# Two-layer transformer: the attention's division queued beside one set of transposes, the next set moved to every second slot

## The chip, the cores and the metric

The kernel runs on one core of a Trainium2 chip. The metric is the device time of one execution in microseconds (us). The core has a matrix engine (TensorE, PE in the profile; its weight loads are listed apart as PEld), a vector engine (VectorE, DVE), a scalar engine (ScalarE, ACT), a general engine (GpSimd, POOL) and a queue for transfers (SyncE, SP). Each engine runs its own list of instructions, and they wait for one another through semaphores.

## The reference, cut to what matters

Four residual steps, each behind a layer norm, over four sequences of 512 positions and 256 features:

```python
x = x + attention0(layernorm(x))      # causal, 16 heads of 16
x = x + mixture0(layernorm(x))        # 8 experts, the best two of each output feature, weighted
x = x + attention1(layernorm(x))      # 16 heads of 128, 4 key heads
x = x + ffn1(layernorm(x))            # gelu(gate) * up, then down, weights of 4 bits
```

The change concerns the first of them:

```python
qkv = einsum('bsd,od->bso', x, w_project)          # then split into q, k, v by head
att = einsum('bhqd,bhkd->bhqk', q, k) / sqrt(16)
att = where(causal, -1e9, att)                     # no key after the query
att = softmax(att, axis=-1)
out = einsum('bhqk,bhkd->bhqd', att, v)
out = einsum('bsd,od->bso', out (heads joined), w_out)
```

The softmax's sum is not taken before the mixing. The values carry a column of ones, so the mixed values come with their own denominators, and the division is made at the end, once for each head and query.

## The kernel before, in words

**Tiling.** The residual `xres` stays on chip as 16 tiles of 128 rows by 256 features. Attention of layer 0 goes by blocks `j` = 0 to 3; a block holds 128 query positions of each of four sequences `s`, and its queries meet the keys of blocks 0 to `j`. Heads are taken four at a time, in groups `g` = 0 to 3. A *batch* is one `(j, s)` with some of its groups: all four in block 0, two in block 1, one in blocks 2 and 3. That makes 4 + 8 + 16 + 16 = 44 batches, numbered `n`.

**What a batch does.** `greatest` (matmuls L614) makes the scores of one batch, `mask` (L629) adds the causal mask to them by matmul and takes each row's greatest on VectorE (L634). `shift` transposes the maxima on TensorE (L645) and subtracts them from the queries on VectorE (L650). `powers` (L664) makes the scores again, transposed, from the shifted queries; ScalarE takes the exponentials (L673) and GpSimd clears what the mask forbids (L683). `mixed` (L700) multiplies with the values, and ScalarE copies the result into `avs` (L708).

**The order of the main work.** The loop over batches writes, for each `n`: scores of `n + 1`, shift of `n`, mask of `n + 1`; a slot; mix of `n - 1`, powers of `n`; a slot.

**The slots.** Everything else is put into these slots by a small planner, `fill`. Each call adds one to the counter `slot` and gives budgets, in microseconds by the author's reckoning, for TensorE and VectorE: 4.0, 2.0, 1.8 or 1.6 for TensorE in the first slot of a batch by block, 4.0, 2.4, 2.2 or 2.0 in the second, and 2.6 for VectorE in each. A budget that was overdrawn is carried on as a debt; one that was left over is not. The other work is a list of *streams*, Python generators. Each piece begins with `yield need(engine, cost, gap, cond)`: it runs once its engine's budget is above zero, `gap` slots have passed since the stream's last piece, and `cond`, if there is one, holds. The streams are asked in the order of the list, again and again, until none can go. The order in which the pieces are written is the order in which TensorE, VectorE and GpSimd carry them out, for their order is taken from the program. At the last batch of a block, slots are added until the next block's inputs are ready, if they are not; after the last batch, slots with 2.0 and 2.6 follow until the last stream of `divided` is done.

**The streams of layer 0.** `prepare` (norm, transposes, projections and values of the next block; its queries and keys go through `stage` and eight transfers into `qk`), `divided` (below), `fold_pieces` (biases folded into router and expert weights `rw` and `ew`), `hidden_pieces` (the norm and the transposes ahead of the mixture), `logit_pieces` and `result_pieces` (the router's and the experts' matmuls, `lg_ps` and `eo`, L226), `weight_pieces` and `addition_pieces` (the mixture's weights and sums on VectorE). What is left of the mixture when layer 0's attention ends goes into the slots of layer 1.

**`divided(j, s)`** is put at the head of the list after the powers of the batch that follows the last batch of `(j, s)`, and so runs 16 times. Its pieces: four transposes of `avs` on TensorE into the PSUM tile `av_T` (L718), which puts the queries on the partitions; a slot later the reciprocal of the denominators (L724) and the product with them (L725), which give `oq`; a slot later two transposes of `oq` into `oq_T` (L733) and ScalarE's copy into `aT` (L736). After the last sequence of a block come the output's matmuls (L745) and the addition to the residual (L754) for two pairs of tiles, and `hidden_pieces(j)` is added to the list.

**PSUM.** Layer 0's scores take turns in five buffers (`ps_sc`), the maxima and the mixed values in one (`ps_mm`). All that the streams make on TensorE takes turns in two buffers, `ps_dn`, with the tag `dn`. A buffer is held until the last reader of its tile is written down in the program, and whoever takes it next waits until that reader is done.

Of the kernel before, what the change touches and what calls it, by code (L numbers as in the profile page):

```python
# [32 lines left out]
def tile_transformer(  # L33
# [75 lines left out]
    slot = 0  # L109

    def need(engine, cost, gap=0, cond=None):
        return engine, cost, gap, cond
# [25 lines left out]
    left = {"PE": 0.0, "DVE": 0.0}  # L138
# [117 lines left out]
    def hidden_pieces(b):  # L256

        out = []
        done = (4 * b - 5, 1)
        last = b == NBLK - 1  # L260
        yield from norm_pieces(b, b1, b2, out, cond=lambda: b < 2 or done in halves)
        xT = b2.tile([P, 2, 512], F32, tag="xT", name=f"xT{b}")
        for hc in range(2):
            yield need("PE", 0.5, 0 if hc else 1 + last)
            ps = transposed(out[0], hc, ps_dn, "dn", f"xT_ps{b}_{hc}")
            ps = ps.rearrange("p t q -> p (t q)")
            if hc:
                nc.scalar.activation(xT[:, hc, :], ps, AF.Identity, bias=last_16)
            else:
                nc.scalar.copy(xT[:, hc, :], ps)  # L270
        normed.clear()
        xTs[b] = xT
# [159 lines left out]
    with ExitStack() as l0:  # L432
# [279 lines left out]
        def divided(j, s):  # L712

            yield need("PE", 0.5, 1)
            avs = avs_of.pop((j, s))
            ps = ps_dn.tile([P, NH0, 32], F32, tag="dn", name=f"av_T{j}_{s}")
            for g in range(4):
                nc.tensor.transpose(  # L718
                    ps[:, 4 * g : 4 * g + 4].rearrange("p h d -> p (h d)"), avs[:, g], ident
                )  # L720
            rden = a2.tile([P, NH0], F32, tag="rden", name=f"rden_{j}_{s}")
            oq = a1.tile([P, NH0, 16], F32, tag="oq", name=f"oq_{j}_{s}")
            yield need("DVE", 0.7, 1)
            nc.vector.reciprocal(rden, ps[:, :, 16])  # L724
            nc.vector.tensor_tensor(  # L725
                oq, ps[:, :, 0:16], rden.unsqueeze(2).to_broadcast([P, NH0, 16]), ALU.mult
            )
            yield need("PE", 0.3, 1)
            if not s:
                aTs[j] = a1.tile([P, 2, 16, NS, 8], F32, tag="aT", name=f"aT{j}")  # L730
            ps = ps_dn.tile([P, 2, P], F32, tag="dn", name=f"oq_T{j}_{s}")
            for k in range(2):
                nc.tensor.transpose(  # L733
                    ps[:, k], oq[:, 8 * k : 8 * k + 8].rearrange("p h d -> p (h d)"), ident
                )
            nc.scalar.copy(aTs[j][:, :, :, s, :], ps.rearrange("p k (g b) -> p k g b", b=8))  # L736
            if s < NS - 1:
                return

            for t in (0, 2):  # L740
                yield need("PE", 1.75, 1)
                ps = ps_dn.tile([P, 2, HID], F32, tag="dn", name=f"o0_{j}_{t}")
                for i in range(2):
                    for k in range(2):
                        nc.tensor.matmul(  # L745
                            ps[:, i],
                            lhsT=aTs[j][:, k, 4 * (t + i) : 4 * (t + i) + 4].rearrange(
                                "p g s b -> p (g s b)"
                            ),
                            rhs=wo[:, k, :], start=k == 0, stop=k == 1,  # L750
                        )
                yield need("DVE", 0.7, 1)
                both = xres[:, 4 * j + t : 4 * j + t + 2, :]
                nc.vector.tensor_tensor(both, both, ps, ALU.add)  # L754
            fold_at = streams.index(fold) if fold in streams else len(streams) - 4
            streams.insert(fold_at, Stream(hidden_pieces(j)))
# [19 lines left out]
        for n in range(NBT):  # L776
# [19 lines left out]
            if n and batches[n - 1][2][-1] == 3:  # L796
                streams.insert(0, Stream(divided(*batches[n - 1][:2])))
# [10 lines left out]
        mixed(NBT - 1)  # L808
        streams.insert(0, Stream(norm_pieces(0, b1, b2, normed_first)))
        last = Stream(divided(*batches[NBT - 1][:2]))  # L810
        streams.insert(0, last)
        while last.next is not None:
# [442 lines left out]
```

## Time and profile before

| | |
|---|---|
| Median of 3 runs | 1215.86 us (1215.13 to 1215.92) |
| The profiled execution's own time | 1213.42 us |
| Its span | 1211.7 us |
| Mean clock granted to TensorE | 0.989 |
| TensorE busy | 1168.9 us, 96% |
| VectorE busy | 802.6 us, 66% |
| ScalarE busy | 485.5 us, 40% |
| GpSimd busy | 121.1 us, 10% |
| L718, transposes of `avs` | 64 matmuls, 10.6 us, 287 ns each |
| L724, reciprocal | 16 times, 4.0 us, 250 ns each |
| L725, product | 16 times, 6.8 us, 424 ns each |
| L733, transposes of `oq` | 32 matmuls, 6.8 us, 293 ns each |
| L736, copy into `aT` | 16 times, 6.4 us, 400 ns each |

The span goes from the first instruction to the last; the profiled execution's own time is a little longer than the span. Layer 0's attention takes the time up to about 420 us. In a row of the timeline, the numbers are the start, the length, then engine, line, operation and the tile written and read, and how many instructions were merged; in brackets stands how long the engine was idle ahead of it, and what ended that. A busy time adds up the recorded lengths. Where TensorE waits in the midst of a group of matmuls, the group's length can grow, and no idle time is shown.

### The profile page before, as it was taken

To read this page: it belongs to the slowest core of one execution; us is meant where nothing else is said; L and a number is where in the kernel's file an instruction comes from. 1 tells how busy PE (TensorE), PEld (TensorE's weight loads), DVE (VectorE), ACT (ScalarE), POOL (GpSimd) and SP (SyncE) were. 2 spreads that over 40 slices of the span, in tenths; PEclk is the share of its full clock that TensorE was granted. 3 is DMA by queue.
4 is the path that set the end of the run, shared out by engine and by line. 5 is a ranking of instruction groups with operands and counts; after the bars stand their busy time and mean duration, and the time that the engine had idled before them with its cause. 6 is when DMAs were issued, how large, how long until landed. Compare 5 with 4: busy or idle time off the path is not lost.

```text
span 1211.7 us, 18780 instructions
## 1 busy us (share of the span) xinstructions
PE 1168.9 (96%) x7278; PEld 679.8 (56%) x7278; DVE 802.6 (66%) x1780; ACT 485.5 (40%) x1101; POOL 121.1 (10%) x155
## 2 busy tenths in 40 slices
PE   6979999999999898999999999999999999999998
PEld 3656555555555543555555555656645456475487
DVE  2555589898887848737886395798499853735710
ACT  1233455664555444434444345355344321312300
POOL 8333321121111000000000000000000000000000
PEclk9899999999999998999999999999999999999999
DMA  7122102000000040000000001021020000000000
GB/s 221 17 56 54 19 4 34 2 1 1 2 1 2 27 147 1 1 1 1 1 1 1 1 1 36 10 55 43 1 62 9 1 1 17 1 1 18 0 1 35
DMA packets 21305, 26.78 MB, mean 22 GB/s; under 512 B 5120, under 2 KB 14592, under 8 KB 21216
## 3 DMA queue, kind: packets, MB, share of 16 engines
q1 hardware_dynamic: 20544, 24.40, 7.6%
q10 hardware_dynamic: 672, 1.18, 0.4%
q8 instruction: 57, 0.93, 0.3%
q14 instruction: 32, 0.26, 0.1%
HBM read 19.27 MB, written 2.10 MB: 18 GB/s over the span
## 4 chain that ended last, share of the span: by engine, by line
PE 81%; DVE 12%; ACT 2%; DMA 2%; issue 1%; SPq 1%; POOL 0%; ACTq 0%; DVEq 0%; POOLq 0%
PE qk_ps L928 10%; PE o L1019 9%; PE y L1175 9%; PE g L856 8%; PE u L856 8%; PE eo L226 8%; PE lg_ps L226 7%; PE s L614 4%; DVE mx L634 3%; PE s L664 3%; PE av L700 2%; PE v_ps L910 2%; PE qk_ps L529 2%; PE s L941 1%; PE a L999 1%
## 5 line engine op out<-in xcount | busy, mean ns | idle before, releaser
L928 PE MATMUL qk_ps<-xT,wqkv 128*128 128x512 f32 x320 | 148.7, 599 | 0.6 <-ACT qT L932 0.6
L226 PE MATMUL lg_ps<-rw,xT 128*128 128x512 f32 x256 | 123.8, 607 | 3.7 <-ACT xT L895 1.7
L226 PE MATMUL eo<-ew,xT 128*128 128x512 f32 x256 | 122.0, 600 | 1.3 <-ACT part L315 1.0
L1019 PE MATMUL o<-wpj,oT 128*128 128x256 f32 x512 | 119.8, 382 | 0.0
L634 DVE TENSOR_REDUCE mx<-s 128x1 f32<-128x384 f32 (+3 forms) x176 | 100.5, 634 | 20.3 <-PE s L629 20.3
L1175 PE MATMUL y<-wd,it 128*128 128x256 f32 x512 | 111.8, 379 | 0.0
L1019 PEld LDWEIGHTS o<-wpj,oT 128*128 128x128 f32 x512 | 95.9, 190 | 28.1 <-issue 15.1
L1175 PEld LDWEIGHTS y<-wd,it 128*128 128x128 f32 x512 | 97.1, 190 | 14.9 <-issue 2.2
L928 PEld LDWEIGHTS qk_ps<-xT,wqkv 128*128 128x128 f32 x320 | 59.3, 190 | 70.0 <-issue 60.2
L673 ACT ACTIVATE pt<-s 128x512 f32<-128x512 f32 (+1 forms) x176 | 83.7, 561 | 34.4 <-PE s L664 34.3
L856 PE MATMUL g<-xT,wgu 128*128 128x512 f32 x192 | 90.4, 593 | 0.0
L856 PE MATMUL u<-xT,wgu 128*128 128x512 f32 x192 | 90.2, 592 | 0.0
L315 ACT ACTIVATE part<-eo,c 128x256 f32<-128x256 f32 x128 | 53.7, 473 | 81.5 <-PE eo L226 76.9
L683 POOL TENSOR_SCALAR_AFFINE_SELECT pt<-pt 128x256 f32<-128x256 f32 (+2 forms) x88 | 55.2, 632 | 268.6 <-ACT pt L673 268.1
L1153 ACT ACTIVATE th<-sq 128x512 f32<-128x512 f32 x64 | 40.3, 629 | 87.6 <-DVE sq L1152 87.6
L177 POOL TENSOR_TENSOR ln_rs<-rs_v,minus_half 128x4 f32<-128x4 f32 x16 | 18.0, 1127 | 563.3 <-DVE rs_v L176 457.9
L226 PEld LDWEIGHTS lg_ps<-rw,xT 128*128 128x128 f32 x256 | 46.5, 192 | 49.0 <-issue 36.9
L226 PEld LDWEIGHTS eo<-ew,xT 128*128 128x128 f32 x256 | 46.4, 190 | 45.8 <-issue 37.0
L614 PE MATMUL s<-qk 32*128 32x128 f32 (+3 forms) x512 | 69.7, 478 | 1.3 <-DMA qk<-stage 0.5
L214 DVE TENSOR_TENSOR xres<-xres,y 128x256 f32<-128x256 f32 x16 | 6.7, 421 | 92.2 <-PE y L1175 92.2
L650 DVE TENSOR_TENSOR qk<-qk,mxT 128x128 f32<-128x128 f32 (+2 forms) x44 | 15.2, 346 | 77.0 <-PE mxT L645 69.3
L289 ACT COPY lg<-lg_ps 128x512 f32<-128x512 f32 x64 | 37.6, 587 | 64.5 <-PE lg_ps L226 64.3
(233 smaller groups left out, 1831.2 us busy)
## 6 DMA issues: line engine op xcount, KB each, us to landing
qk<-stage SPq DMA_DIRECT2D x56, 64.0 KB, 2.4
wqkv<-in_w_qkv SPq DMA_DIRECT2D x8, 320.0 KB, 6.0
rw<-in_router_w SPq DMA_DIRECT2D x8, 256.0 KB, 4.8
ew<-in_expert_w SPq DMA_DIRECT2D x8, 256.0 KB, 5.0
wpj<-in_w_proj SPq DMA_DIRECT2D x1, 2048.0 KB, 11.9
out<-xres SPq DMA_DIRECT2D x4, 512.0 KB, 2.6
xres<-in_x SPq DMA_DIRECT2D x3, 512.0 KB, 8.1
dq_wgu<-in_gate_w SPq DMA_DIRECT2D x8, 128.0 KB, 2.4
```

The lines of the kernel that those rows point to most:

```text
L226: nc.tensor.matmul(ps, lhsT=xT[:, hc, (g % 4) * P : (g % 4 + 1) * P], rhs=w[:, hc, 2 * pair : 2 * pair + 2, :].rearrange("p e o -> p (e o) ...
L289: nc.scalar.copy(lg[:, 2 * pair : 2 * pair + 2, :].rearrange("p e o -> p (e o)"), ps)
L315: nc.scalar.mul(part[:, e % 4], ps[:, i], c[:, e : e + 1])
L614: nc.tensor.matmul(tiles[h][:, b * nk : (b + 1) * nk].rearrange("p (c k) -> p c k", k=P), lhsT=queries(j, g)[r, s], rhs=qk[r, g, : j + 1, ...
L634: nc.vector.tensor_reduce(maxes[n % 2][:, :nb, h, 0], ps[:, : nb * nk].rearrange("p (b k) -> p b k", b=nb), AX.X, ALU.max,)
L673: nc.scalar.activation(pt[:, i, : nb * nk], tiles[2 * pair + i][:, : nb * nk], AF.Exp, scale=0.25)
L683: nc.gpsimd.affine_select(out=last, in_=last, compare_op=ALU.is_ge, fill=0.0, base=0, pattern=pattern, channel_multiplier=-1,)
L856: nc.tensor.matmul(ps, lhsT=wgu[:, w, half, jj, par * P : (par + 1) * P], rhs=xT[:, half, :], start=half == 0, stop=half == 1,)
L928: nc.tensor.matmul(ps, lhsT=wqkv[:, hc, kv, h, :], rhs=xT[:, hc, :], start=hc == 0, stop=hc == 1,)
L1019: nc.tensor.matmul(ys[t // 2][:, t % 2], lhsT=state["o"][:, h, t * P : (t + 1) * P], rhs=wpj[:, HPK * kv + h, :], start=kv == 0 and h == 0 ...
L1153: nc.scalar.activation(th, sq, AF.Tanh, scale=0.7978845608028654)
L1175: nc.tensor.matmul(ps, lhsT=it[:, c // 2, c % 2, t * P : (t + 1) * P], rhs=wd[:, c // 2, c % 2, :], start=c == 0, stop=c == 2 * NJ - 1,)
```

## The change

In `divided`, three lines differ. The piece that made the division no longer yields: reciprocal and product are written down directly behind the transposes of `avs`, in the same slot, and 0.7 is taken off VectorE's budget by hand, so that the budget may go below zero. The piece with the transposes of `oq` keeps its cost of 0.3 and its gap of one slot, counted now from the transposes of `avs`, and gets a condition: the number of the slot has to be odd. Since the counter begins at 0, the first slot of the first batch, behind a mask, has the number 1.

```diff
                 nc.tensor.transpose(
                     ps[:, 4 * g : 4 * g + 4].rearrange("p h d -> p (h d)"), avs[:, g], ident
                 )
+
             rden = a2.tile([P, NH0], F32, tag="rden", name=f"rden_{j}_{s}")
             oq = a1.tile([P, NH0, 16], F32, tag="oq", name=f"oq_{j}_{s}")
-            yield need("DVE", 0.7, 1)
+            left["DVE"] -= 0.7
             nc.vector.reciprocal(rden, ps[:, :, 16])
             nc.vector.tensor_tensor(
                 oq, ps[:, :, 0:16], rden.unsqueeze(2).to_broadcast([P, NH0, 16]), ALU.mult
             )
-            yield need("PE", 0.3, 1)
+
+            yield need("PE", 0.3, 1, cond=lambda: slot % 2)
             if not s:
                 aTs[j] = a1.tile([P, 2, 16, NS, 8], F32, tag="aT", name=f"aT{j}")
```

## The prediction

> **What bounds the kernel now.** I read the page's totals first, then the busy time by stretch of layer 0, then TensorE's timeline with the idle time ahead of each row, last VectorE's rows around the same moments.
>
> ```profile
> PE 1168.9 (96%) x7278; PEld 679.8 (56%) x7278; DVE 802.6 (66%) x1780; ACT 485.5 (40%) x1101; POOL 121.1 (10%) x155
> ...
> PE 81%; DVE 12%; ACT 2%; DMA 2%; issue 1%; SPq 1%; POOL 0%; ACTq 0%; DVEq 0%; POOLq 0%
> ```
>
> TensorE sets the end: 1168.9 of 1211.7 us busy and 81% of the chain. No matmul is removed, so what can shrink or grow is its idle 42.8 us, and waits that hide inside stretched rows. Where that idle time lies (columns: stretch, length, busy time of PE, PEld, DVE, ACT, POOL, granted clock, DMA share, GB/s):
>
> ```profile
> 42.00:92.00 50.00, 40.54 (x481) 27.71 (x480) 28.75 (x55) 16.58 (x32) 18.00 (x16) 0.94 0.20 43
> 92.00:162.00 70.00, 66.03 (x784) 41.27 (x786) 40.26 (x86) 29.22 (x60) 24.67 (x26) 0.97 0.15 32
> 162.00:290.00 128.00, 123.89 (x1252) 68.03 (x1245) 112.68 (x287) 72.19 (x205) 21.65 (x35) 1.00 0.06 10
> 290.00:427.00 137.00, 132.29 (x1285) 72.93 (x1282) 115.30 (x273) 70.34 (x184) 17.11 (x32) 0.99 0.05 15
> ```
>
> The four stretches in which the edited helper runs hold 9.5, 4.0, 4.1 and 4.7 us of idle PE. TensorE's timeline, picked rows (start, length, row, idle before it and what ended it):
>
> ```profile
> 64.60 0.66 PE L718 MATMUL av_T<-ident,avs 128*128 128x128 f32 x4
> 65.09 0.38 PE L733 MATMUL oq_T<-ident,oq 128*128 128x128 f32 x2
> 67.13 1.99 PE L529 MATMUL qk_ps<-xT,wp 128*128 128x512 f32 x4 [1.65 <-ACT aT L736]
> ...
> 84.03 0.44 PE L733 MATMUL oq_T<-ident,oq 128*128 128x128 f32 x2 [1.81 <-DVE oq L725]
> 84.93 0.38 PE L244 MATMUL fold<-rows 128*128 128x512 bf16 x1 [0.46 <-ACT aT L736]
> ...
> 114.67 0.38 PE L244 MATMUL fold<-rows 128*128 128x512 bf16 x1 [1.30 <-DVE oq L725]
> ...
> 199.41 0.66 PE L202 MATMUL xT_ps<-ident,xn 128*128 128x128 f32 x4 [1.23 <-ACT aT L736]
> ```
>
> Two sorts of wait. At 84.03 the divided values' transposes wait for a late division: on VectorE it stands behind four reductions and four batch-norm pairs, and ends at 83.97. At 67.13 and 114.67 a matmul that does not read the division waits for a buffer. The pool `dn` has two. `av_T` keeps one from its transposes until the division, which is emitted a slot later; everything emitted between runs through the other one alone, each product waiting for the evacuation of the last. At 67.13 the projection could take only the buffer of `oq_T`, so it waited for the copy `aT`.
>
> **What the Trainium skill says.** PSUM — Partial Sum Buffer, section Engine vs sequencer instructions: VectorE's queue is strictly first in, first out, and matmuls complete in program order; the trace agrees (the division at 83.27 comes after all eight batch-norm rows, though its data were there at 82.2). The same page, Specifications (TRN2): eight banks per partition; score 5, `mm` 1 and `dn` 2 are all of them, so no third `dn` buffer relieves this. Perfetto Trace Analysis, section Optimization Strategy: a gap that repeats on the engine that should be full can mean no buffer for the next tile; idle times of 0.68, 0.67, 0.68 and 0.67 at 51.60, 58.63, 91.22 and 93.01 fit. TensorE: Matmul & The Clock Gate, section What's actually happening: idling for a window of about 3.4 us halves the array's clock; here the clock is 0.50 from 86 to 94, where one group of 32 `av` matmuls took 1.94 us against 1.08; but the longest single gap before it is 1.81, so the trace agrees in kind only.
>
> **The change, part by part.** Each batch has two slots: the first (odd number) behind the mask, the second (even) behind the powers. The count starts at 0, and the loops at block ends add no slot in the order the trace shows, so parity holds through all 44 batches. Before, a group's av_T goes into even slot k, its division into k+1, its oq_T into k+2. Now the division is queued in k and oq_T goes into k+1. The last group (slots 89, 90, 91) keeps its place, since 90 is even: 15 of 16 move.
>
> *Removed waits, 42 to 100 us.* Buffer: 0.68 (51.60), 0.67 (58.63), 1.65 (67.13) = 3.00. Late: 0.16 + 0.56 (74.67, 75.86), 1.81 + 0.46 (84.03, 84.93), 1.31 (89.46), 0.68 (91.22), 0.67 (93.01), 0.38 (99.40) = 6.03. Not all can be kept. The scores at 76.20 need eight transfers whose queries leave at 69.1 and land near 76; the projection moves by 3.00, so I allow 3.0 there, and the 0.72 at 74.67 and 75.86 is lost to the transfers. Next VectorE limits: from the shift at 78.21 to that at 89.23 it works nearly without a gap. The same work in the new order (reductions 2.4, statistics 2.2, rs_v 0.2, fold 1.3, division 0.7, normalising 3.5) saves only the 0.58 wait for POOL, which fold and division now cover. So 3.0 + 0.6 + 0.68 + 0.38, and half of 0.67: 5.0 kept of 9.0.
>
> *92 to 162 us.* 1.30 at 114.67 goes (VectorE idles 3.71 before the shift at 111.18, so the division can run at once). Of 0.68 + 0.78 + 0.16 at 130 to 132 I take half, since oq_T joins that crowded slot: 2.1.
>
> *162 to 410 us.* At 164.80 powers waited 1.80 for the shift, which stood behind VectorE's filler. The division's 0.7 is now debited one slot earlier, so one 1.22 us subtraction leaves that slot: 1.22 - 0.67 = 0.5. Further 0.25 (167.38), 1.23 (199.41), twice 0.16: 2.3. The wait of 0.73 at 410.86 is the last group's and stays.
>
> *Added.* oq_T (0.44 a pair) lay behind the powers, where scalar exponentials still hold the score buffers that the next scores need; its time there was partly free. Score groups of block 3 take 1.14 us undisturbed, but 3.21, 2.42, 3.16 and 3.35 at 305.34, 315.15, 363.73 and 389.43: the wait is inside the row. Of the seven pairs from 197 to 388, two stand ahead of such stretched groups and others are near: 3 x 0.44 = 1.3. In slot 24 the 0.3 of planner budget set free lets one more product in early, and slot 26 loses one, so its scores meet the exponentials uncovered: 0.7, an estimate from these stretches.
>
> *At nothing.* VectorE does the same work. The division (0.25 + 0.42) now waits at the head of its slot for av_T; behind it stand that slot's filler, the next shift and its reductions. A stall there is covered by VectorE's wait for the next maxima's transpose: in 10 of the 15 cases VectorE sat idle before that shift (7.31, 6.93, 2.50, 3.71, 2.88, 5.05, 2.66, 0.60, 2.17, 2.11 us). In the other five, cover gone, it costs at most 0.67 each = 3.4, less what the earlier debit holds back; I take 0, and keep -3.4 in the range. The copy `aT` (0.41) moves ahead of the exponentials, where ScalarE is mostly idle. No DMA is added; those behind the projections leave earlier by what these move. Output products and hidden(0) may start a slot earlier, but folded weights and first products stay bound to slot 19; layer 1 gets the same work.
>
> Sum: -5.0 - 2.1 - 2.3 + 1.3 + 0.7 = -7.4 us. Against the profiled execution's own 1213.42 (span 1211.7) that is 1206.0. The shown runs' median is 2.4 higher: 1215.86 - 7.4 = 1208.5.
>
> **Rivals.** *More is kept, and the clock stays up.* Idle PE around 84 to 92 costs the half clock for 10.2 us; in it av (+0.86), mask (+0.45), two normed transposes (+0.88), powers (+0.37) and small rows (+0.7) lost 3.3. With 2 of the 4.0 withheld also kept: 1208.5 - 5.3 = 1203. For: two waits of that gap go. Against: the normalised rows themselves stay VectorE's.
>
> *Hidden anyway.* Transfers to 76 and VectorE's run to 89 hold the early start, and the later exposures eat the rest: 1215.
>
> *Slower.* oq_T comes out from under the exponentials in all 15 groups: 15 x 0.44 = 6.6, while the early stretch gives back only about 3.5: 1219. It decides once exposed time passes the kept waits. Against: 10 of the 14 score groups from 161 to 259 take their undisturbed 0.93, so there is no wait there to pay unless they stood within 0.44 of one.
>
> *It doesn't do what it says.* If parity flipped at a block end, oq_T would stay in its old slot and only the buffer part (about 3) would come: 1212.5.
>
> **How the numbers follow.** Likeliest 0.60, with 1205.5 to 1212 as its own range; the larger gain 0.17; parity 0.03; hidden 0.12; slower 0.08. Measurement tells about 0.2% = 2.4 us from nothing. Faster: 0.60 + 0.17 + 0.03 = 0.80; same 0.12; slower 0.08. The range 1202.5 to 1215.0 holds the likeliest, most of the larger gain and a part of hidden.
>
> **What would show it.** Right: division rows next to av_T on VectorE, before the shift; no PE wait on oq at 84 and 114; the projection after av_T at full pace; oq_T after mask rows; idle PE in 42 to 92 near 5 instead of 9.5. Wrong: new PE waits of powers on the shift, score groups stretched behind the groups' powers, or the transfers' wait growing near 73 to 76. Another half-clock stretch elsewhere (3.3 each) would also break the number.

## The result, and the profile after

The median fell from 1215.49 us to 1204.49 us (six runs of each): ratio 0.9924, with a 95% interval of 0.9898 to 0.995. The same kernel, run again beside the experiments, had 1205.89 us against 1212.61: 0.995 (0.9934 to 0.9966). The profiled execution took 1203.68 us with a span of 1202.0 and a mean clock of 0.993, where before had 1213.42, 1211.7 and 0.989. The two profiles differ by 9.7 us.

The page after, its totals and the shares of the chain by engine:

```profile
PE 1161.8 (97%) x7278; PEld 676.9 (56%) x7278; DVE 804.8 (67%) x1780; ACT 488.4 (41%) x1101; POOL 124.2 (10%) x155
...
PE 82%; DVE 11%; DMA 2%; ACT 2%; issue 1%; POOL 0%; SPq 0%; ACTq 0%; DVEq 0%; POOLq 0%
```

TensorE still sets the end. Its idle time went from 42.8 us to 1202.0 - 1161.8 = 40.2, and its 7278 matmuls take 7.1 us less, so that most of the gain lies inside rows, not between them (1.0 of it in the six matmuls ahead of the first batch, which took 5.46 and 4.48 us). A row is also longer where the granted clock is lower, and before ran at half clock for longer; what that makes is estimated below, at the rival on the clock. The busy time by stretch, in the columns used before:

```profile
42.00:92.00 50.00, 46.89 (x561) 32.45 (x558) 28.01 (x56) 20.78 (x40) 18.62 (x17) 0.97 0.20 44
92.00:162.00 70.00, 66.16 (x776) 41.89 (x773) 48.51 (x105) 30.61 (x65) 25.23 (x25) 1.00 0.12 24
162.00:290.00 128.00, 126.70 (x1285) 69.59 (x1288) 113.21 (x280) 72.65 (x203) 21.87 (x35) 1.00 0.06 10
290.00:427.00 137.00, 125.69 (x1193) 67.56 (x1185) 110.99 (x275) 73.57 (x195) 16.45 (x28) 1.00 0.12 40
```

In the first stretch TensorE is idle for 3.1 us instead of 9.5, and 561 matmuls end in it instead of 481; in the third for 1.3 instead of 4.1. The last line can't be set beside before's: by then the kernel is ahead, and the stretch reaches into the start of layer 1 (its share of transfers rose from 15 to 40 GB/s).

The timeline of TensorE after, picked rows (start, length, row, idle time before it and what ended that):

```profile
52.69 3.62 PE L551 MATMUL v_ps<-wp,xT 128*128 128x256 f32 x16
...
60.29 0.66 PE L718 MATMUL av_T<-ident,avs 128*128 128x128 f32 x4
61.84 1.96 PE L529 MATMUL qk_ps<-xT,wp 128*128 128x512 f32 x4 [0.90 <-DVE oq L726]
...
78.87 0.61 PE L629 MATMUL s<-later,ident_h 128*128 128x128 bf16 x8
79.62 0.44 PE L735 MATMUL oq_T<-ident,oq 128*128 128x128 f32 x2
80.40 0.30 PE L202 MATMUL x_ps<-ident,xn 128*128 128x128 f32 x1 [0.34 <-DVE xn L186]
82.20 1.89 PE L202 MATMUL x_ps<-ident,xn 128*128 128x128 f32 x7 [1.50 <-DVE xn L186]
...
388.80 1.08 PE L700 MATMUL av<-pt,va 128*32 128x128 f32 x32 [1.34 <-DVE qk L650]
...
393.93 2.52 PE L700 MATMUL av<-pt,va 128*32 128x128 f32 x32 [1.03 <-ACT pt L673]
...
407.49 1.99 PE L747 MATMUL o<-wo,aT 128*128 128x256 f32 x8 [1.06 <-DVE xres L756]
```

The lines of the edited helper now have other numbers: division L725 and L726, `oq_T` L735, copy L738, output L747, addition L756. At 52.69 two groups of values run as one row; before, the second had waited 0.67 us for a buffer at 58.63. At 61.84, behind the transposes at 60.29, stands the projection that had waited 1.65 us at 67.13 for the copy `aT`; it now waits 0.90 for the product `oq`, that is, for `av_T`'s own buffer. At 79.62 `oq_T` comes directly behind the mask without a wait, where at 84.03 it had waited 1.81. In its place TensorE waits 0.34 and 1.50 us for the normalised rows `xn`. The last three rows are waits at the end of layer 0's attention that are new or longer than before. VectorE after, around the third group:

```profile
69.82 0.26 DVE L725 RECIPROCAL rden<-av_T 128x16 f32<-128x16 f32 x1
70.11 0.42 DVE L726 TENSOR_TENSOR oq<-av_T,rden 128x256 f32<-128x256 f32 x1
72.59 0.42 DVE L650 TENSOR_TENSOR qk<-qk,mxT 128x256 f32<-128x256 f32 x1 [2.06 <-PE mxT L645]
```

The division stands ahead of the shift, and VectorE is idle for 2.06 us after it: the early division had room there.

**Where in time the gain arises.** I take the start of the maxima's transposes (L645) of batch `n` in before, less that of the same batch in the other kernel, and set this *lead* to zero at batch 1, because the edit first acts in slot 4. At batch 1 the change was 2.2 us ahead already, from its start-up; in the second profile of the same kernel it was 0.3. So 2.2 of the 9.7 us are not the edit's, and 7.5 are. From batch 1 to the first transposes of `avs` the lead of the kernels in the table moves by 0.0 to 0.8 us, although none of the edits has acted there; leads that differ by less than 1 us are therefore not told apart. Batches 6, 12, 25 and 43 start in before at 102.4, 155.0, 252.0 and 400.5 us, the first scores of layer 1 at 450.7.

| Lead over before, us | n = 6 | 12 | 25 | 43 | layer 1 begins | end | so layer 1 |
|---|---|---|---|---|---|---|---|
| change | 8.1 | 6.0 | 8.6 | 11.2 | 7.6 | 7.5 | -0.1 |
| change, second profile | 7.3 | 5.3 | 7.7 | 10.4 | 6.9 | 6.8 | -0.1 |
| division alone | 6.5 | 7.5 | 7.9 | 8.5 | 6.1 | 11.8 | +5.7 |
| early, but buffer held | 3.9 | 2.3 | 2.3 | 2.8 | 0.1 | 5.8 | +5.7 |
| debit alone | 4.0 | 2.3 | 2.0 | 1.5 | -0.4 | 5.2 | +5.6 |
| no mask | 8.1 | 6.1 | 8.6 | 13.3 | 11.4 | 12.5 | +1.1 |
| change, buffer held | 4.8 | -3.3 | -2.3 | -11.7 | -15.3 | -16.1 | -0.8 |
| division and addition | 6.5 | 8.5 | 8.1 | 11.1 | 11.5 | 16.5 | +5.1 |
| no mask and addition | 8.6 | 9.0 | 7.7 | 10.6 | 10.3 | 14.2 | +3.9 |

All of the change's gain is in layer 0's attention, and 3.6 us of it are given back between batch 43 and layer 1. Slot numbers in what follows come from the program's planner; the traces don't hold them.

### The profile page after: what moved, and what is told of

Read it like the earlier page. It is cut to its first block, busy times and chain, and to the rows that moved or that the text cites. A ratio compares the mean times of both kernels' runs of the same rounds, so it can differ in the third digit from the quotient of the medians.

```text
span 1202.0 us, 18779 instructions
## 1 busy us (share of the span) xinstructions
PE 1161.8 (97%) x7278; PEld 676.9 (56%) x7278; DVE 804.8 (67%) x1780; ACT 488.4 (41%) x1101; POOL 124.2 (10%) x155
## 4 chain that ended last, share of the span: by engine, by line
PE 82%; DVE 11%; DMA 2%; ACT 2%; issue 1%; POOL 0%; SPq 0%; ACTq 0%; DVEq 0%; POOLq 0%
PE qk_ps L930 10%; PE o L1021 9%; PE y L1177 9%; PE g L858 8%; PE u L858 8%; PE lg_ps L226 8%; PE eo L226 8%; PE s L614 4%; PE s L664 3%; DVE mx L634 3%; PE v_ps L912 2%; PE av L700 2%; PE qk_ps L529 2%; PE s L943 1%; PE a L1001 1%; DVE xn L186 1%
## 5 line engine op out<-in xcount | busy, mean ns | idle before, releaser
L683 POOL TENSOR_SCALAR_AFFINE_SELECT pt<-pt 128x256 f32<-128x256 f32 (+2 forms) x88 | 58.2, 666 | 257.2 <-ACT pt L673 257.1
L614 PE MATMUL s<-qk 32*128 32x128 f32 (+3 forms) x512 | 66.8, 479 | 1.3 <-ACT pt L673 0.7
L1156 DVE SCALAR_TENSOR_TENSOR th<-th,g 128x512 f32<-128x512 f32 x63 | 43.2, 685 | 29.2 <-ACT th L1155 29.2
## 6 DMA issues: line engine op xcount, KB each, us to landing
wpj<-in_w_proj SPq DMA_DIRECT2D x1, 2048.0 KB, 11.8
```

What stands on the lines that cost most here:

```text
L614: nc.tensor.matmul(tiles[h][:, b * nk : (b + 1) * nk].rearrange("p (c k) -> p c k", k=P), lhsT=queries(j, g)[r, s], rhs=qk[r, g, : j + 1, ...
L683: nc.gpsimd.affine_select(out=last, in_=last, compare_op=ALU.is_ge, fill=0.0, base=0, pattern=pattern, channel_multiplier=-1,)
L1156: nc.vector.scalar_tensor_tensor(th, th, 1.0, gp, ALU.add, ALU.mult)
```

## The experiments

The question was which of the two sorts of wait that the prediction named (late division, held buffer) carries the gain, and whether the moved transposes and their condition add to it.

**1. The division alone.** (Edit against the kernel before.) The division is queued as in the change; `oq_T` stays in its old slot. The earlier debit moves fillers of VectorE, but ahead of slot 91 only one piece of TensorE: a matmul of `fold` goes from slot 10 to 9.

```diff
-            yield need("DVE", 0.7, 1)
+            left["DVE"] -= 0.7
...
-            yield need("PE", 0.3, 1)
+            yield need("PE", 0.3, 2)
```

> Only the division is queued with the transposes of avs; the transposes of oq stay in their old slots (gap of two, no condition), and no other piece moves. Theory (an early division frees a buffer and is never waited for): most of the gain is here. Kept are the waits of 0.68, 0.67, 0.56, 1.81, 0.67, 1.30 and some of the rest; lost are those that stem from oq_T crowding its slot (0.46, 0.38, 1.23) and 0.5 for the shift: ratio to before 0.994 to 0.997, that is 4 to 7 us faster. Rival (the place of oq_T makes the gain): at most 2 us faster, ratio 0.998 to 1.000.

Measured: 1201.97 us, ratio 0.991 (0.9894 to 0.9925), more than expected and not slower than the change. Timeline of TensorE in this kernel:

```profile
64.56 0.44 PE L735 MATMUL oq_T<-ident,oq 128*128 128x128 f32 x2 [2.09 <-ACT stage L533]
65.45 1.98 PE L529 MATMUL qk_ps<-xT,wp 128*128 128x512 f32 x4 [0.46 <-ACT aT L738]
...
82.75 0.41 PE L735 MATMUL oq_T<-ident,oq 128*128 128x128 f32 x2 [2.48 <-DVE rw L250]
```

The waits of 0.68 and 0.67 at 51 and 58 us are gone, and at 82.75 TensorE waits no more for `oq`. But `oq_T` still stands where it did, and waits for whoever has the other buffer. Layer 0 gains 6.1, a little less than with the change; layer 1 gains 5.7, which I hadn't foreseen (experiment 5).

**2. The transposes alone.** (Against the kernel before.) The division stays where it was; `oq_T` goes into the first odd slot from then on, which is the division's own (but for block 3's first group, slot 73 instead of 67).

```diff
-            yield need("PE", 0.3, 1)
+            yield need("PE", 0.3, 0, cond=lambda: slot % 2)
```

> The division stays a slot late, behind the reductions on VectorE; the transposes of oq go into the slot behind the mask, right after it is queued. Theory: TensorE now waits for the reductions (1.95 to 2.48 us) and the division (0.67) in nearly each of 14 groups, 2 to 3 us each with nothing put ahead, in part recovered by later slack: 15 to 35 us slower, ratio 1.012 to 1.03. Rival (the place of oq_T makes the gain): 3 us or more faster than before.

Measured: 1269.3 us, ratio 1.0462 (1.0442 to 1.0483), a much greater loss than expected. The waits of TensorE from 40 to 470 us (in all, times, longest), then one row of its timeline, then the busy time of a stretch:

```profile
PE oq_T L733 <- DVE oq L725: 45.1, 13, 5.4
```

```profile
100.16 0.66 PE L733 MATMUL oq_T<-ident,oq 128*128 128x128 f32 x2 [3.18 <-DVE oq L725]
```

```profile
42.00:92.00 50.00, 37.47 (x417) 26.92 (x418) 20.92 (x46) 14.31 (x27) 12.98 (x11) 0.84 0.20 43
```

Thirteen times TensorE waits for a division that stands behind the shift, 3.5 us each, and then runs at a lower clock: 0.84 in that stretch, 0.961 over the whole. So the early slot of `oq_T` is a loss unless the division is early too.

**3. No mask.** Only the condition is left out of the change, so that `oq_T` comes in the slot after `av_T`, whatever its number.

```diff
-            yield need("PE", 0.3, 1, cond=lambda: slot % 2)
+            yield need("PE", 0.3, 1)
```

> The change without its condition on the slot's number. Only two groups go elsewhere: block 3's first (slot 68 instead of 73) and the very last (slot 90 instead of 91, so the output's pieces come a slot earlier). Theory: the condition itself is worth nothing, ratio to before as with the change, 0.990 to 0.994, within 2.5 us of it. Rival (it matters that oq_T never stands behind the powers): 3 us or more slower than the change.

Measured: 1200.75 us, ratio 0.990 (0.9881 to 0.992). Up to batch 25 its leads are those of the change within 0.1 us; then they reach 13.3 at batch 43 and 11.4 at layer 1, against 11.2 and 7.6. So the condition acts from block 3 on only, and the profile without it is 5.0 us better at the end. Whether the condition costs time is not settled by the times: against the change's first ratio, 0.9924 (0.9898 to 0.995), the intervals overlap, against its second, 0.995 (0.9934 to 0.9966), they do not. Set beside the division alone, from which it differs by the earlier `oq_T` and what the planner moves for it, it is 5.3 us further ahead when layer 1 begins (11.4 against 6.1), but only 0.7 at the end, for it gains 1.1 in layer 1 instead of 5.7. So the moved transposes do gain in layer 0, beside the early division; over the whole the intervals of the two kernels overlap.

**4. The change with the buffer held.** A copy of one column of `av_T`, written down behind the copy `aT`, keeps its buffer up to there (edit against the change); it adds 16 copies of 128x1.

```diff
             yield need("PE", 0.3, 1, cond=lambda: slot % 2)
+            held = ps
...
+            last_use = a2.tile([P, 1], F32, tag="held", name=f"held_{j}_{s}")
+            nc.vector.tensor_copy(last_use, held[:, 0, 16:17])
```

> The change, with one reading more: VectorE copies a single column of av_T behind the transposes of oq, a slot later, so that the buffer of av_T is held about as long as before while the division is early. No other piece moves. Theory (buffer and lateness both count): the waits for a buffer come back, some 0.68, 0.67, 0.68, 0.67 and 1.30 in blocks 0 and 1, and the 16 copies cost about 0.1 each off the path: 3 to 5 us of the gain are lost, ratio to before 0.995 to 0.998. Rival (only the late division counts): within 1.5 us of the change.

Measured: 1228.18 us, ratio 1.0121 (1.0102 to 1.014): some 23 us worse than the change, where 3 to 5 were expected, and 16 worse than before (1212.09). Rows of VectorE and of TensorE:

```profile
109.13 0.15 DVE L741 COPY held<-av_T 128x1 f32<-128x1 f32 x1
```

```profile
109.43 0.66 PE L736 MATMUL oq_T<-ident,oq 128*128 128x128 f32 x2 [2.62 <-DVE held L741]
```

This copy belongs to the same group as the `oq_T` below it. On VectorE it stood behind the four reductions; until it was done it held the buffer of `av_T`, an output product held the second one, and TensorE stood for 2.62 us with none. Behind that the clock was at half, and the next group of values took 3.75 us instead of 1.99. This holds the buffer in another place than the kernel before did, so it shows what happens when both are held, not what the old holding cost; where the rest of the 23 us lies was not followed up. The next experiment was made for the old holding.

**5. Early but held, and the debit alone.** Both leave every piece of layer 0 but the division itself in the slots of experiment 1. In the first (edit shown against experiment 1, whose gap of two slots is split in two) the division is early, but a one-column copy of `av_T` holds the buffer until the division's old slot; it adds 16 copies of 128x1. In the second the division stays in its old slot, and only the planner's debit of 0.7 is taken early.

```diff
...
-            yield need("PE", 0.3, 2)
+            yield need("DVE", 0.0, 1)
+            last_use = a2.tile([P, 1], F32, tag="held", name=f"held_{j}_{s}")
+            nc.vector.tensor_copy(last_use, ps[:, 0, 16:17])
+            yield need("PE", 0.3, 1)
```

```diff
-            yield need("DVE", 0.7, 1)
+            left["DVE"] -= 0.7
+            yield need("DVE", 0.0, 1)
```

> The division queued early as in the run of the division alone, the transposes of oq in their old slots, and one reading more: VectorE copies one column of av_T in the slot in which the division used to stand, so the buffer of av_T comes free where it did before. No piece of TensorE moves against the kernel before or against the division alone. Theory (the buffer makes the larger part): the waits for a buffer are back and only those for the late division are gone (some 0.56 + 1.81 and what hangs on them): ratio to before 0.996 to 1.001. Rival (only the late division counts): as with the division alone, 0.989 to 0.993.

> The kernel before, with one thing changed: the division's 0.7 is taken off VectorE's budget a slot earlier, beside the transposes, while the division itself stays where it was. Its order is that of the run with the early division and the held buffer in every slot but for the division. Theory (that run's gain of 0.4% is not the early division but the planner's other order of layer 1, which the last group's debit sets off): ratio to before 0.995 to 0.998, the end of layer 0's attention where it was before, and about 5.7 us gained behind it. Rival (the early division made it): ratio 0.999 to 1.001.

Measured: early but held 1208.94 us, ratio 0.9964 (0.995 to 0.9978); debit alone 1207.74, ratio 0.9952 (0.9936 to 0.9969). TensorE with the early division and the held buffer:

```profile
50.78 1.98 PE L529 MATMUL qk_ps<-xT,wp 128*128 128x512 f32 x4 [0.68 <-ACT stage L533]
57.81 1.99 PE L551 MATMUL v_ps<-wp,xT 128*128 128x256 f32 x8 [0.68 <-ACT va L557]
66.31 1.98 PE L529 MATMUL qk_ps<-xT,wp 128*128 128x512 f32 x4 [1.66 <-ACT aT L741]
82.65 0.89 PE L718 MATMUL av_T<-ident,avs 128*128 128x128 f32 x4 [1.93 <-DVE held L732]
88.83 0.66 PE L202 MATMUL x_ps<-ident,xn 128*128 128x128 f32 x4 [0.68 <-ACT xT L571]
```

The waits of 0.68, 0.67, 1.65 and 0.68 in the kernel before are all back, and the 1.81 for `oq` at 84.03 has become 1.93 for the held buffer. Layer 0 ends at +0.1 with the early division and at -0.4 with the late one. So an early division that doesn't free the buffer is worth nothing that can be told here, and the release, which apart from the small copies is all that sets experiment 1 apart (every engine whose order the program fixes has the same order in both), is worth 6.0 us of layer 0 (0.1 to 6.1), and in the ratio 0.9964 to 0.991. The clock doesn't make this difference: from 50 to 440 us both kernels run at half clock three times for 3.4 us (from 84.4, 357.5 and 384.8 us with the release, from 82.9, 362.8 and 390.1 without).

Both gain 5.6 to 5.7 us in layer 1, as experiment 1 does. That is another order of the work there, which comes from the planner: with the debit of the last group taken in slot 89 instead of 90, VectorE ends the mixture's weights of one tile in slot 90 instead of 91, a product of the mixture falls into slot 91 instead of 92, what follows moves up, and the program needs 252 slots instead of 254. The number of slots alone doesn't make the gain: no mask needs 252 too and gains 1.1 there. The stretch from 450 to 490 us, in before and then with the debit alone:

```profile
450.00:490.00 40.00, 35.14 (x180) 17.62 (x179) 31.45 (x86) 16.36 (x42) 2.38 (x2) 0.91 0.00 1
```

```profile
450.00:490.00 40.00, 37.41 (x199) 20.34 (x198) 30.64 (x81) 16.48 (x42) 1.06 (x1) 1.00 0.00 0
```

And the rows in it where TensorE takes up the last transposes and the router's matmuls, in before and with the debit alone:

```profile
478.56 1.12 PE L202 MATMUL xT_ps<-ident,xn 128*128 128x128 f32 x4 [2.04 <-ACT lg L289]
481.35 3.78 PE L226 MATMUL lg_ps<-rw,xT 128*128 128x512 f32 x4 [1.67 <-ACT xT L895]
```

```profile
469.38 1.71 PE L202 MATMUL xT_ps<-ident,xn 128*128 128x128 f32 x8 [0.73 <-ACT th L382]
471.41 1.98 PE L226 MATMUL lg_ps<-rw,xT 128*128 128x512 f32 x4 [0.32 <-ACT xT L896]
```

Waits of 2.04 and 1.67 shrink to 0.73 and 0.32, and the router's group takes 1.98 instead of 3.78, at full clock; before, 6.8 us of the stretch were at half. The change takes its last debit in slot 89 too, but by then VectorE has one piece of these weights more left to do, so that they end in slot 91 as in before. Its TensorE work stands in before's slots from slot 89 on, and it gets none of the gain.

**6. The addition treated alike.** The addition to the residual holds the output's buffer over a slot in the same manner. Here its debit too is taken by hand and it is queued behind its output product: once with the division alone, once with no mask.

```diff
-                yield need("DVE", 0.7, 1)
+                left["DVE"] -= 0.7
```

> The division alone, and the same done to the other result that holds a buffer of the pool over a slot: the addition of the output's product to the residual is queued with its matmuls, 8 times. Theory of the buffer: 0 to 4 us faster than the division alone (ratio to before 0.988 to 0.991), because products beside the output find two buffers; VectorE then waits about 2 us for the matmuls, at most 8 times, mostly under its wait for the maxima. Rival (VectorE's stalls at the head of its queue count): 3 us or more slower than the division alone.

> The change without its condition, with the addition to the residual queued at the output's matmuls as well. If the place of oq_T is worth nothing, it comes out like the division with the sum, within 2.5 us; if moving oq_T is worth 2 us or more, it is the fastest of the four by that.

Measured: with the division alone 1196.86 us, ratio 0.9866 (0.985 to 0.9882), faster than the change, with the lowest median of all; its gain over the division alone is a little above the 0 to 4 us expected. With no mask 1201.8, ratio 0.9908 (0.9888 to 0.9928), no better than without the addition. The two outputs of a block, division alone, then with the addition:

```profile
96.39 1.95 PE L747 MATMUL o<-wo,aT 128*128 128x256 f32 x8
105.85 1.95 PE L747 MATMUL o<-wo,aT 128*128 128x256 f32 x8
...
403.67 1.89 PE L747 MATMUL o<-wo,aT 128*128 128x256 f32 x8
410.01 1.99 PE L747 MATMUL o<-wo,aT 128*128 128x256 f32 x8
```

```profile
96.56 1.95 PE L747 MATMUL o<-wo,aT 128*128 128x256 f32 x8
101.26 1.89 PE L747 MATMUL o<-wo,aT 128*128 128x256 f32 x8
...
401.21 1.89 PE L747 MATMUL o<-wo,aT 128*128 128x256 f32 x8
404.95 1.99 PE L747 MATMUL o<-wo,aT 128*128 128x256 f32 x8
```

The second output follows after 4.7 and 3.7 us instead of 9.5 and 6.3. The lead at layer 1 rises from 6.1 to 11.5, and nearly all of that comes late: at batch 25 it is 7.9 and 8.1, at batch 43 8.5 and 11.1. Part of it is clock: the two stretches at half clock from 357.5 and 384.8 us are gone, which at most makes half of their 6.8 us. It helps with one order of the work and not with the other; why the other loses 2.2 us between batches 12 and 31, I didn't find; a stretch at half clock from 275.4 us on, 3.4 us long, makes at most 1.7 of it.

**7. Which group pays for the condition.** The change again, and the change with the condition waived for one group: the last, `(3, 3)`, which the condition keeps in slot 91, and the first of block 3, `(3, 0)`.

```diff
-            yield need("PE", 0.3, 1, cond=lambda: slot % 2)
+            yield need("PE", 0.3, 1, cond=lambda: slot % 2 or (j, s) == (3, 3))
```

```diff
-            yield need("PE", 0.3, 1, cond=lambda: slot % 2)
+            yield need("PE", 0.3, 1, cond=lambda: slot % 2 or (j, s) == (3, 0))
```

> The changed kernel as it is, beside the others on one chip. Ratio to before 0.990 to 0.994; against the earlier runs of the division alone (0.991) the place of oq_T is worth less than 2.5 us either way.

> The change with its condition waived for the very last group alone (slot 90 instead of 91). Theory (what the condition costs is the tail: output and everything behind it come a slot later, and layer 1 is ordered otherwise): as without the condition, ratio to before 0.988 to 0.992. Rival (it is block 3's first group, put off to slot 73): as the change, 0.993 to 0.997.

> The change with its condition waived for block 3's first group alone (slot 68 instead of 73); layer 1 is ordered as before. Theory of the tail: as the change, ratio to before 0.993 to 0.997. Rival (block 3's first group): 0.988 to 0.992.

Measured: the change again 1205.89 us, 0.995 (0.9934 to 0.9966); last free 1203.21, 0.9918 (0.9895 to 0.9941); first free 1204.69, 0.9923 (0.9906 to 0.9941). Inconclusive: both intervals reach into that of the change and that of no mask. By the profiles the leads at the end are 8.8 and 7.9 against 7.5, together 1.7 more, where no mask has 5.0 more; the two do not add up to it. These leads hold clock as well: first free ran at half clock from 157.5 and from 355.5 us on, for 3.4 us each, where the change did not.

## Why the prediction was right, and where it was wrong

**The sum.** Predicted 7.4 us; the profiles show 7.5 from the point where the edit first acts, 6.8 in the second profile. The median of 1208.5 was set beside 1215.86; measured were 1204.49 and 1205.89 beside 1215.49 and 1212.61, 11.0 and 6.7 less. The first difference may hold start-up luck such as the 2.2 us seen in the profile.

**"Two sorts of wait: a late division, a held buffer."** Half right. The held buffer is shown: experiment 5 puts all of the gain that the early division has in layer 0 on the release, 6.0 us in the order of experiment 1. That it is worth as much in the change's own order, beside the moved transposes, was not measured. The lateness is no cause by itself: the wait at 84.03 moved over to the buffer when only the division came early. The repeating gaps of 0.67 and 0.68 were what the prediction took them for, with the section Optimization Strategy of the Trainium skill's Perfetto Trace Analysis: no buffer for the next tile.

**"-5.0 from 42 to 100 us" and "-2.1 from 92 to 162".** Together 7.1; the lead at batch 12 is 6.0 (5.3 in the second profile). The 8.1 at batch 6 were not all time won, since outputs and projections stand in other places by then. Of the terms, the waits at 51, 58, 84 and 114 are gone, and `xn` became the limit as the prediction said (0.34 and 1.50). Only the 1.65 at 67.13, counted as removed, left 0.90: the buffer is free only when the division is done, and the projection comes right behind `av_T`. "Idle PE near 5" was 3.1.

**"-2.3 from 162 to 410".** From batch 12 to 25 the lead grows by 2.6. The 1.80 that powers waited for the shift at 164.80 shows as 0.67 for `oq` and 0.40 for the shift at 154 and 155. The 1.23 at 199.41 didn't go: it came back as 1.22 at 189.19, at another matmul of the mixture.

**"+1.3, `oq_T` comes out from under the exponentials", "+0.7 in slot 24".** The first had the wrong sign as far as the profile shows. On the page the score groups (L614) take 66.8 us in 512 matmuls instead of 69.7, and the lead grows by 2.6 from batch 25 to 43. Of these, 1.5 are clock: before ran at half clock from 393.2 us on for 3.4 us, and a mixing group took 1.94 us there instead of 1.08, powers 1.77 instead of 1.17. Of the second nothing is seen: the lead passes from 6.0 at batch 12 to 8.6 at 25.

**Not foreseen: the end of layer 0.** From batch 43 to layer 1 the lead falls from 11.2 to 7.6. The rows at 388.80, 393.93 and 407.49 show it: TensorE waits 1.34 for the shift, 1.03 for the exponentials ahead of a group of 2.52, and 1.06 for the residual addition. The two mixing groups in before:

```profile
401.26 1.08 PE L700 MATMUL av<-pt,va 128*32 128x128 f32 x32 [0.47 <-DVE qk L650]
...
405.29 2.21 PE L700 MATMUL av<-pt,va 128*32 128x128 f32 x32
```

The shift was waited for there too, 0.47, and the last group was stretched to 2.21. So the change loses 0.87, 1.34 and 1.06, together 3.3 of the 3.6. Between the last two shifts VectorE has an addition of the mixture in place of a subtraction, and one piece more of the mixture's weights; that the shift is late because of them is likely, but no run singles it out. In experiment 6, where the addition is not put off, the lead doesn't fall there.

**"15 of 16 move; parity holds."** Parity holds, but 14 moved. The first group of block 3 went from slot 68 to 73: TensorE's budget was used up in slots 67, 69 and 71, and the condition forbids the even ones. After, its `av_T` is at 299.05, its `oq_T` at 329.87. This is what the condition costs in place; in time it could not be told (experiment 7).

**"At nothing: the division at the head of VectorE's queue."** Right. VectorE waited six times, 11.9 us in all, for `av_T`, but in the five of these that a shift follows it still waited 1.89 to 4.41 us for the maxima then, and the sixth is the last group's. From 40 to 420 us the shift's waits and those for `av_T` together went from 76.1 to 67.1 us. This is the answer on the tile `av_T` of the change, engine idle before it until (us, times):

```profile
  PE av_T L718: 11.9, 6
```

**The rival "more is kept, and the clock stays up"** came in part. The half clock from 86.0 us on lasted 10.2 us in before; after, it is 3.4 us from 83.0 on, and the shorter stretch at 393 is gone. Before (two lines), after, and the debit alone, in the columns of the stretches:

```profile
85.97:96.21 10.24, 7.58 (x75) 5.00 (x72) 7.94 (x13) 1.54 (x3) 1.68 (x1) 0.50 0.01 2
393.17:396.58 3.41, 3.25 (x58) 2.69 (x60) 3.41 (x6) 0.27 (x1) 0.00 (x0) 0.50 0.00 0
```

```profile
82.97:86.38 3.41, 3.41 (x42) 2.31 (x42) 3.41 (x7) 1.17 (x2) 0.00 (x0) 0.50 0.02 5
```

```profile
83.91:87.32 3.41, 3.41 (x28) 2.41 (x27) 3.36 (x6) 0.37 (x1) 1.98 (x2) 0.50 0.00 0
```

By the prediction's sum the first stretch cost 3.3; a busy stretch of 3.4 costs at most half of it, 1.7. With the 1.5 at 393, some 3 us of the change's lead at batch 43 are clock, an estimate from these rows. The shorter half clock near 84 doesn't need the early division: the debit alone has it too, and is 4.0 us ahead at batch 6, with the division late and the buffer held. That lead is gone again when layer 1 begins (-0.4).

So the likeliest case came out at the right size by luck, with errors that cancel: its 7.1 us up to batch 12 were 6.0, clock included, and its 0.3 after that (2.3 - 1.3 - 0.7) were 5.2 up to batch 43, again with clock, less 3.6 at the end, 1.6. **"Layer 1 gets the same work"** holds for the change (-0.1), but hangs on one slot: where the debit at slot 89 lets the tile's weights end in slot 90 (experiments 1 and 5), it is worth 5.7 us there.

## What to carry to other kernels

Where much work passes through a pool of two buffers, try the last reader of a tile directly behind its writer, even if nobody waits for its result: here the release was worth 6.0 us, and the early result without the release nothing. A short wait that repeats at matmuls which don't read the delayed value is the sign of it; look for the tile that is kept over other work, and then for the next tile treated so (the addition gave another 0.4% in one order of the work, and nothing in the other). In a planner with budgets, the time of a debit alone can reorder work far away, so what an edit wins in its own place, what it wins by reordering and what it wins by a higher clock should be told apart.

## What the runs showed of the hardware

- The half clock came in stretches of 3.4, 6.8 and 10.2 us (in before from 393.2, 478.5 and 86.0 us on), and the longest single gap in the 5 us ahead of the longest was 1.81 us. After the change 0.34 and 1.50 us of idle time at 80 and 82 us were still followed by one of 3.4 us, in which TensorE was busy throughout and a group of 32 mixing matmuls took 1.94 us instead of 1.08.
- Two profiles of the same kernel differed by 1.9 us at batch 1, before any edited piece had run (2.2 and 0.3 us ahead of before). A gain of this size is read better between two points inside the trace than from the spans.
